# Order of the first loads and place of the second layer's constants in the spectral stage of a two-layer metaformer kernel

## The chip, the cores and the metric

The kernel runs on one core of one Trainium2 chip. The metric is the device time of one execution in microseconds, given as the median of three runs. The profile is one further execution; its own time stands in the table below. A difference under 0.2% (some 5 us here) can hardly be told from no change.

## The reference, cut to what matters

The input is a batch of 8 images with 128 channels and 32 by 32 positions, which become 1024 tokens per image. Layer 0 is a row attention and then a spectral unit (STU). Layer 1 is a deformable convolution along rows and then a mixture of eight experts.

```python
x = x + _L0_conv_ref(_ln_c(x), ...)            # attention, softmax over one row of 32 keys
t = _to_tokens(x)
t = t + _L0_ffn_ref(_ln_t(t), sigma, phi, M_u, M_phi_plus, M_phi_minus, log_weights, gumbel)
x = x + _L1_conv_ref(_ln_c(x), conv_w, ...)    # gather at learned offsets, 3 taps
t = t + _L1_ffn_ref(_ln_t(t), router_w, ...)   # top 2 of 8 experts
```

The change lies in how the spectral unit starts. The spectral unit convolves the tokens causally with 16 filters (the columns of `phi`), for even and odd time steps, multiplies each result by 128 by 128 matrices (`M_phi_plus`, `M_phi_minus`, weighted by `sigma` and by a choice of four resolutions), and adds three plain lags with the matrices `M_u`. The kernel writes the convolution as products with Toeplitz blocks of the filter.

## The kernel before, in words

**Stages.** `attention_bounded` (from line 500) runs first, for all eight images, and stores its result in DRAM as `x1d` (line 688). Then `spectral_and_second_layer` (line 1589) runs everything else in one order that is written out by hand: Tile keeps this order on every engine (`manual_schedule`). The spectral products and the second layer of the image before are interleaved there.

**The loop.** The work is a list of 128 pairs n = (image b, filter k), 16 filters for each of 8 images. Each pair has two halves, `src` 0 and 1, and each half two slots. In a half, `filter_image` (line 1514) makes three groups of matrix products: `p_x` in slot 0, `p_y` in slot 1, `p_z` after it. ScalarE copies `p_x` out (lines 1555, 1556), GpSimd adds the copies into `part` (line 1557), VectorE adds `part` to `p_y` and `p_z` (lines 1562, 1565, 1572). The filter of a pair is the tile `teto` (three buffers), its block differences are `diff` (lines 1299 and 1300, on GpSimd). `mix` (line 1509) then multiplies the convolved tokens `us` with the matrices `mf` and sums in PSUM (`po`). Pair m = n-2 is mixed in half 0 (its term 1), pair m = n-1 in half 1 (its term 0). So the first mix stands in half 1 of pair 1 and needs `mf` of pair 0.

**The matrices.** For the first 16 pairs `mf` is made on the core: `load_parts` (line 1426) brings both source matrices into one buffer, `m_room`; `terms` (lines 1431, 1432, GpSimd) makes their sum and difference, `both`, in one buffer; `weigh` (lines 1439 and 1441, VectorE) makes `mf`, which is also stored to DRAM (line 1444). `between` sets when: after half 0 of pair n come the differences of filter n+1 and `weigh(n)`; after half 1 come `terms` for pair n+1 and the load of `m_room` for pair n+2. Pair 0 is special: `terms(0)` comes after its half 0, `weigh(0)` and `terms(1)` after its half 1. At the end of a pair the filter for n+3 is loaded.

**Side work.** `rows[0]` is a queue of generators. `advance` (line 1611), called after every slot, adds 3.2 units to a budget and runs steps of the generator at the head until the budget is spent; a step costs what it yields, or 1 unit. So a pair has 12.8 units. The queue starts with `channels` of image 0 (line 1460: transposes `p_ut`, memset and copies into `ut`, which has one buffer), and `layer.setup()` (line 821), which makes the second layer's constants in 22 steps: ten small loads into `gw` (lines 830 to 843), three into `bias` (847, 849), memsets and iotas (851 to 864), twelve stores of zeros into `tab` (871), `shift` tiles, `cb`, `rw`, `rb`, `ew`, and eight small loads into `ebm` (902). At pair 1 `begin(1)` is put behind it: `prepare(1)`, then the `channels` of image 1. `add_lags` (line 1497) multiplies `ut` of image 0 by the lag matrices `mu` in half 1 of pair 2. The second layer of image 0 starts after pair 17.

**Queues.** All direct loads and stores are issued by SyncE (SP) in program order. The program gives SP's transfers eight completion semaphores in turn, so a transfer is issued only when the one eight places before it has landed. `prepare` (line 1446) issues a gather of `x1` on GpSimd. Before the loop SP issues, in this order, `teto` of pairs 1 and 2 (the filter of pair 0 was read during the attention), the four loads of `mu`, and `m_room` of pair 0.

Of the kernel before, what the change touches and what calls it, by code (L numbers as in the profile page):

```python
# [1587 lines left out]

def spectral_and_second_layer(tc, spec, layer, weights):
    work = [(b, k) for b in range(B) for k in range(NF)]  # L1590
    imgs = {0: spec.prepare(0)}
    filters = {0: spec.given.filter, 1: spec.load_filter(1), 2: spec.load_filter(2)}
    less = {0: spec.given.given.diff}
    spec.load_lags()

    mf = {}
    parts = spec.load_parts(0)
    both = None

    rows = [deque([spec.channels(imgs[0], layer.bank), layer.setup()]), deque()]
    starts = {}
    todo = [0.0, 0.0]

    def second_layer(b, x1):
        got = []
        yield from layer.points(b, imgs[b]["x2"], got, False, x1)
        rows[1].append(layer.sampled(b, got, False))

    def advance(time):
        for r, row in enumerate(rows):
            todo[r] = todo[r] + time if row else 0.0
            while todo[r] > 0 and row:
                took = next(row[0], row)
                if took is row:
                    row.popleft()
                else:
                    todo[r] -= took or 1.0

    def between(n, src):

        nonlocal parts, both
        if src == 0 and n + 1 < len(work):
            less[n + 1] = spec.differences(filters[n + 1])
        if n == 0:
            if src == 0:
                both = spec.terms(parts)
                parts = spec.load_parts(1)
                return  # L1630
            mf[0] = spec.matrices()
            spec.weigh(0, both, mf[0])
        elif n < NF and src == 0:
            mf[n] = spec.matrices()
            spec.weigh(n, both, mf[n])
        if src == 1 and n + 1 < NF:
            both = spec.terms(parts)
            if n + 2 < NF:
                parts = spec.load_parts(n + 2)
        if n in (0, 1) and src == 1 - n:  # L1640
            spec.lags(weights, range(2 * n, 2 * n + 2))

    sums = {}
    for n in range(len(work) + 2):
        now = work[n] if n < len(work) else None
        if now is not None:
            b, k = now
            if k == 1 and b + 1 < B:  # L1650
                starts[b + 1] = spec.begin(b + 1, layer.bank, imgs)
                rows[0].append(starts[b + 1])
            elif k == 0 and b:
                for _ in starts[b]:
                    pass
            us = sums[n] = spec.sb.tile([C, 2, 2, HT], F32, tag="us", name="us", bufs=3)
        for src in range(2):
            run = iter(())
            if now is not None:
                run = spec.filter_image(imgs[b], src, filters[n], less[n], us, layer.bank)  # L1660
            for slot, spans in enumerate((SPANS[0:3], SPANS[3:4])):
                next(run, None)
                m = n - 2 + src
                if 0 <= m < len(work):
                    img, k = imgs[work[m][0]], work[m][1]
                    if src == 1 and slot == 0 and k == 0:
                        spec.start_sums(img)
                    if src == 1 and slot == 0 and k == NF - 3:
                        img["tokens"] = layer.residual(img["b"])
                    if src == 1 and slot == 0 and k == 1:  # L1670
                        spec.add_lags(img)
                    spec.mix(img, 1 - src, spans, mf[m], sums[m], k == NF - 1)
                    if src == 0 and slot == 1 and k == NF - 1:
                        spec.finish(img)
                        if img["b"] + 1 < B:
                            rows[0].appendleft(second_layer(img["b"], img["tokens"]))
                if now is not None:
                    advance(RATE if b + 1 < B else LAST_RATE)
            next(run, None)
            if now is not None:  # L1680
                between(n, src)
        if n + 3 < len(work):
            filters[n + 3] = spec.load_filter(work[n + 3][1])
        if NF <= n + 2 < len(work):
            mf[n + 2] = spec.read_matrices(work[n + 2][1])

    last = imgs[B - 1]
    runs = [layer.image(B - 1, last["x2"], last["tokens"]), chain(*rows[0], *rows[1])]
    while runs:
        runs = [r for r in runs if next(r, r) is not r]  # L1690
# [3 lines left out]
def metaformer_kernel(  # L1694
# [41 lines left out]
    with tc.manual_schedule(engines=None):  # L1736
        spectral_and_second_layer(tc, spec, layer, weights)
# [50 lines left out]
```

## Time and profile before

| what | value |
|---|---|
| median of three runs | 2662.8 us (2657.89 to 2663.11) |
| profiled execution | 2658.17 us, of which the span is 2656.4 us |
| TensorE busy | 2500.7 us, 94% |
| VectorE, ScalarE, GpSimd busy | 1852.6, 1064.2, 1449.2 us |
| mean granted TensorE clock | 0.978 |
| attention's last TensorE work | ends at 908.57 us of the span |
| first product of the spectral stage | 911.79 us |

Each engine runs its own instructions in order, and the page gives its busy time. An idle time stands in square brackets behind an instruction in the timeline, with the work that ended it. TensorE's products are the longest row, so its idle times in the span and its granted clock tell where time is lost.

### The profile page before, as it was taken

The page shows a single profiled execution, that of the slowest core. Times are in us where ns is not written, and L with a number is a line of the kernel's source. Part 1 is how long each engine was busy: PE and PEld are TensorE (multiplying, and loading weights), DVE is VectorE, ACT ScalarE, POOL GpSimd, SP SyncE. Part 2 cuts the span into 40 slices and gives each one's busy share as a digit, 9 for nine tenths or more (in the row PEclk, how much of TensorE's full clock was granted, in tenths as well). Part 3 has the DMA queues.
Part 4 walks back from the last instruction along what each step waited for, and adds up shares of the span by engine and source line. Part 5 has one row for each costly group of instructions (what it writes and reads, how often), then busy time and mean ns, then how long its engine had stood idle before and what let it go on. Part 6 is the DMA issues. An engine that isn't in the chain of part 4 may idle for free. (4 is left out here: it accounts for less than half of the span.)

```text
span 2656.4 us, 47332 instructions
## 1 busy us (share of the span) xinstructions
PE 2500.7 (94%) x18768; PEld 1750.2 (66%) x18768; DVE 1852.6 (70%) x2800; ACT 1064.2 (40%) x1982; POOL 1449.2 (55%) x1535
## 2 busy tenths in 40 slices
PE   6999999999999789999999999999999999999924
PEld 3555555555555468878778778778778778778612
DVE  3788888888888545549749748658658658658656
ACT  4676766667766311124214214224224224224222
POOL 4777777877778555446246237237337337236230
PEclk9999999999999999999999999999999999999966
DMA  1000000000000154465365266266356357256160
GB/s 30 2 18 2 18 17 2 18 2 18 10 18 18 57 165 157 145 191 176 99 189 180 91 182 192 87 183 188 98 168 201 100 154 215 92 144 213 48 182 20
DMA packets 214531, 271.29 MB, mean 102 GB/s; under 512 B 20948, under 2 KB 147092, under 8 KB 214304
## 3 DMA queue, kind: packets, MB, share of 16 engines
q1 hardware_dynamic: 197504, 212.61, 26.6%
q0 software_dynamic: 16800, 55.59, 6.3%
q8 instruction: 150, 2.46, 0.4%
q14 instruction: 77, 0.63, 0.1%
HBM read 200.22 MB, written 67.92 MB: 101 GB/s over the span
## 5 line engine op out<-in xcount | busy, mean ns | idle before, releaser
L623 POOL TENSOR_TENSOR t<-e 128x1024 f32<-128x1024 f32 x256 | 608.2, 2376 | 198.9 <-ACT e L614 198.7
L651 DVE TENSOR_TENSOR e<-e,rb 128x2048 f32<-128x2048 f32 x256 | 570.8, 2277 | 84.5 <-PE rb L644 84.5
L614 ACT ACTIVATE e<-s 128x2048 f32<-128x2048 f32 x256 | 481.1, 1879 | 253.0 <-PE s L609 250.5
L1557 POOL TENSOR_TENSOR part<-us,part 128x256 f32<-128x256 f32 x256 | 191.0, 746 | 705.6 <-ACT part L1556 698.7
L1509 PE MATMUL po<-us,mf 128*128 128x128 f32 (+2 forms) x2048 | 528.1, 381 | 5.8 <-DVE mf L1441 5.8
L1555 ACT COPY us<-p_x 128x256 f32<-128x256 f32 x256 | 95.2, 372 | 753.8 <-PE p_x L1544 740.6
L1562 DVE TENSOR_TENSOR part<-p_y,part 128x512 f32<-128x512 f32 x256 | 175.3, 685 | 289.3 <-PE p_y L1544 200.2
L1509 PEld LDWEIGHTS po<-us,mf 128*128 128x128 f32 x2048 | 308.8, 191 | 37.8 <-DVE mf L1441 6.2
L609 PE MATMUL s<-q,k 32*128 32x256 f32 x4096 | 295.9, 403 | 15.2 <-ACT e L614 14.4
L661 PE MATMUL av<-e,vt 128*32 128x256 f32 x4096 | 288.2, 389 | 4.0 <-DVE e L651 2.7
L1572 DVE TENSOR_TENSOR us<-p_z,part 128x512 f32<-128x512 f32 x256 | 174.8, 683 | 159.3 <-PE p_z L1544 159.2
L609 PEld LDWEIGHTS s<-q,k 32*128 32x128 f32 x4096 | 186.4, 185 | 137.9 <-ACT e L614 116.6
L1544 PEld LDWEIGHTS p_z<-diff,gap 128*128 128x128 f32 x1024 | 191.9, 189 | 125.3 <-issue 87.5
L1544 PE MATMUL p_z<-diff,gap 128*128 128x256 f32 x1024 | 263.4, 379 | 3.1 <-DVE base L907 3.1
L661 PEld LDWEIGHTS av<-e,vt 128*32 128x32 f32 x4096 | 101.4, 109 | 141.6 <-issue 84.7
L1091 POOL DMA_INDIRECT g<-tab,here x168 | 165.9, 988 | 43.2 <-issue 37.0
L1109 ACT ACTIVATE g<-g,w 128x128 f32<-128x128 f32 x448 | 140.1, 393 | 74.2 <-DMA g<-tab,here 73.2
L1299 POOL TENSOR_TENSOR diff<-teto 128x516 f32<-128x516 f32 x127 | 165.0, 1299 | 2.2 <-DMA teto<-in_phi_o 1.4
L1117 DVE TENSOR_REDUCE x<-g 128x128 f32<-128x1536 f32 x56 | 158.7, 2834 | 5.0
L637 DVE RECIPROCAL r<-z 128x256 f32<-128x256 f32 x64 | 112.5, 1757 | 71.3 <-PE z L630 71.1
L1544 PE MATMUL p_y<-diff,gap 128*128 128x256 f32 x512 | 152.9, 380 | 2.4 <-POOL diff L1299 2.3
L1544 PE MATMUL p_x<-teto,ht 128*128 128x256 f32 x512 | 131.4, 379 | 0.0
(268 smaller groups left out, 3708.9 us busy)
## 6 DMA issues: line engine op xcount, KB each, us to landing
mf<-mfd SPq DMA_DIRECT2D x112, 512.0 KB
tab<-gs SPq DMA_DIRECT2D x192, 256.0 KB
teto<-in_phi_o SPq DMA_DIRECT2D x127, 256.5 KB
teto<-in_phi_e SPq DMA_DIRECT2D x127, 256.0 KB
mfd<-mf SPq DMA_DIRECT2D x16, 512.0 KB
xc<-in_x SPq DMA_DIRECT2D x8, 512.0 KB
x1d<-xt SPq DMA_DIRECT2D x8, 512.0 KB
m_room<-in_M_plus SPq DMA_DIRECT2D x16, 256.0 KB
```

The costliest lines, as they stand in the source:

```text
L609: nc.tensor.matmul(s[:, j, c, :], img["k"][rows, hg, 2 * r + c, :], q[rows, qc * QU : (qc + 1) * QU], start=True, stop=True,)
L614: nc.scalar.activation(e.rearrange("p j c q -> p (j c q)"), s.rearrange("p j c q -> p (j c q)"), AF.Exp, scale=float(HD) ** -0.5,)
L623: nc.gpsimd.tensor_add(t, e[:, :, 0, :], e[:, :, 1, :])
L651: nc.vector.tensor_tensor(e, e, un["rb"].unsqueeze(2).to_broadcast([P, NH, 2, QU]), ALU.mult)
L661: nc.tensor.matmul(qrt["av"][32 * j : 32 * j + 32, 0:QU], img["v"][:, 2 * r + c, P * hg + 32 * j : P * hg + 32 * j + 32], un["e", r][:, j, ...
L1091: nc.gpsimd.indirect_dma_start(out=tiles[-1][:, tap].rearrange("p k c -> p (k c)"), out_offset=None, in_=rows[tap], in_offset=bass.Indirec ...
L1299: lambda: nc.gpsimd.tensor_sub(blocks[:, :, 0:2], pair, one),
L1509: self.nc.tensor.matmul(out, lhsT, rhs, start=bank not in img["opened"], stop=last, skip_group_check=True)
L1544: nc.tensor.matmul(out, weights, moving, start=start, stop=stop, skip_group_check=True)
L1557: nc.gpsimd.tensor_add(part[:, 0], mine[:, :, 0:P], part[:, 1])
L1562: nc.vector.tensor_tensor(part[:, 2:4], y[:, 0].unsqueeze(1).to_broadcast([C, 2, 2, P]), part[:, 0:2], ALU.add)
L1572: nc.vector.tensor_tensor(result(2, 4), z, part[:, 2:4], ALU.add)
```

## The change

The loads ahead of the loop are put in another order. `load_parts(0)` comes first, then the filter of pair 1, then `prepare(0)` and the four loads of `mu`, and the filter of pair 2 last. In `rows[0]` a generator that yields 40.0 once stands between `channels` of image 0 and `layer.setup()`, so that 40 units of the budget pass with no step. Nothing is added to or left out of the computation. Everything behind the filler in `rows[0]` moves with it: the constants now start in half 0 of pair 3 and end in half 1 of pair 4, `prepare(1)` stands in half 1 of pair 4 and `channels` of image 1 in half 0 of pair 5. Before, the constants ran from half 0 of pair 0 to half 1 of pair 1, and `channels` of image 1 in half 1 of pair 1 and half 0 of pair 2.

```diff
 def spectral_and_second_layer(tc, spec, layer, weights):
     work = [(b, k) for b in range(B) for k in range(NF)]
-    imgs = {0: spec.prepare(0)}
-    filters = {0: spec.given.filter, 1: spec.load_filter(1), 2: spec.load_filter(2)}
-    less = {0: spec.given.given.diff}
-    spec.load_lags()
 
     mf = {}
     parts = spec.load_parts(0)
     both = None
-
-
-
-    rows = [deque([spec.channels(imgs[0], layer.bank), layer.setup()]), deque()]
+    filters = {0: spec.given.filter, 1: spec.load_filter(1)}
+    less = {0: spec.given.given.diff}
+    imgs = {0: spec.prepare(0)}
+    spec.load_lags()
+    filters[2] = spec.load_filter(2)
+
+
+
+    rows = [deque([spec.channels(imgs[0], layer.bank), iter([40.0]), layer.setup()]), deque()]
     starts = {}
     todo = [0.0, 0.0]
```

## The prediction

> **What bounds the kernel.** I read the page first.
>
> ```profile
> span 2656.4 us, 47332 instructions
> PE 2500.7 (94%) x18768; PEld 1750.2 (66%) x18768; DVE 1852.6 (70%) x2800; ACT 1064.2 (40%) x1982; POOL 1449.2 (55%) x1535
> PE   6999999999999789999999999999999999999924
> ```
>
> TensorE (PE) is the long row. Of its 40 slices of 66.4 us it has one dip inside the span, the 14th and 15th, where attention ends and the spectral stage begins. The table of stretches, for PE alone, cuts this start:
>
> ```profile
> core 0: us, PE busy (x), PEclk, DMA share, GB/s
> 911.80:926.70 14.90, 14.89 (x68) 0.89 0.74 212
> 926.70:932.50 5.80, 0.00 (x0) 0.72 0.12 1
> 932.50:936.10 3.60, 3.57 (x10) 0.50 0.22 56
> 936.10:946.10 10.00, 8.47 (x43) 1.00 0.83 262
> 946.10:949.20 3.10, 0.04 (x1) 1.00 1.03 274
> 949.20:953.20 4.00, 3.99 (x11) 0.57 0.61 233
> 961.00:1095.00 134.00, 134.00 (x622) 1.00 0.52 165
> 1095.00:2500.00 1405.00, 1392.66 (x6452) 1.00 0.50 154
> ```
>
> PE idles 5.8 us, 1.5 us inside the fourth row, and 3.1 us, and runs two pieces at about half clock. From 961 to 2500 it idles 12.3 us of 1539. What is won at the start should therefore stay won. The timeline names the causes:
>
> ```profile
> 919.10 1.28 POOL L1299 TENSOR_TENSOR diff<-teto 128x516 f32<-128x516 f32 x1 [0.28 <-DMA teto<-in_phi_o]
> 925.84 1.27 POOL L1431 TENSOR_TENSOR both<-m_room 128x512 f32<-128x512 f32 x1 [4.76 <-DMA m_room<-in_M_minus]
> 929.87 0.40 SPq L1426 DMA_DIRECT2D m_room<-in_M_plus  x1
> 932.53 2.08 PE L1509 MATMUL po<-us,mf 128*128 128x128 f32 x6 [5.84 <-DVE mf L1441]
> 938.55 1.26 POOL L1431 TENSOR_TENSOR both<-m_room 128x512 f32<-128x512 f32 x1 [8.87 <-DMA m_room<-in_M_minus]
> 958.98 0.59 ACT L1471 COPY ut<-p_ut 128x512 f32<-128x512 f32 x1 [27.87 <-PE po L1509]
> ```
>
> PE's first mix waits for `mf` of pair 0, that for `both`, that for `m_room`, which stood last on SP. The next `m_room` needs 8.7 us from issue to use. ScalarE stands 27.9 us before image 1's `ut` copy, since `ut` has one buffer and image 0's lags come later. The transfers of 928 to 935 us show why the second `m_room` is late, and 921 to 924 us give the rate of 512-byte pieces:
>
> ```profile
> DMA packets 913, 0.03 MB, mean 4 GB/s; under 512 B 903, under 2 KB 903, under 8 KB 913
> ...
> DMA packets 2079, 1.04 MB, mean 345 GB/s; under 512 B 77, under 2 KB 2074, under 8 KB 2079
> ```
>
> For 7 us almost nothing moved but the constants' 4-byte pieces (`bias`), with `m_room` already issued behind them.
>
> **What the Trainium skill says.** "DMA: Bandwidth & Descriptors", Queues, rings and completion order: the transfers of one issuer share one row of rings, and each DMA engine takes descriptors in ring order. The 7 us above agree. The same page, Rules for kernel authors: a strided last dimension becomes one descriptor per element; `bias` and `gw` agree (903 pieces under 512 B). "TensorE: Matmul & The Clock Gate", What's actually happening: after an idle window of about 3.4 us the clock halves until a busy one has passed. The trace half agrees: 3.1 us of idle time was enough at 946, the 1.43 us at 941 to 943 was not. The same page's section on the array's architecture calls ACT and DVE strict FIFO; the ScalarE line shows it.
>
> **The change part by part.** All on the profiled execution, in its microseconds.
>
> *SP's first issue.* `teto` waited 2.9 us for the landing of `x1d` by the waits of SP, and went at 913.46. `m_room` now takes the place in SBUF where `x1` stood, so it may not have that wait; no engine starts the stage before 911.8. Between 911.8 and 913.5 I take 913.0.
>
> *`m_room` first.* It is 1024 pieces of 512 B: 1.5 us at 2079 pieces in 3 us. `teto` of pair 1 was released at 919.1 after an issue at 913.46; now 1.5 later for `m_room` and 0.5 earlier for the issue: 920.1 (918.9 to 921.1, if the `x1` gather hits it for half a microsecond more). On GpSimd, in order: `diff` 1.28 + 0.74, `both` 1.27 + 1.26 (`m_room` landed long before), `part` 0.72: 920.1 + 2.0 + 2.5 + 0.7 = 925.3. Before, from that `part`'s end at 929.0 to PE's mix at 932.53 took 3.5 us (VectorE's three adds and `weigh`). So the mix comes at 928.8 (927.6 to 929.8); PE runs out of work at 926.7 as before, and idles 2.1 us instead of 5.8. A half-clock window of 3.4 us costs 1.7; with 2.1 between the two gaps above I take half of it, 0.9 (0 to 1.7).
>
> *`mu` and the second filter behind.* `mu` (1536 pieces, 2.3 us) lands by about 923.5, the filter (3 to 4 us) by about 928. VectorE wants `mu` after `weigh`, at 928.8, GpSimd the filter after about 931. Cost nothing; were that cover gone, each would cost its own lateness. `prepare(0)` stays first on GpSimd's stage: nothing.
>
> *Constants away from pairs 0 and 1.* GpSimd's 2.9 us of memsets and iotas lay under the wait for `teto`: nothing. But SP now issues the second `m_room` right after `both`, about 924.7, behind the filter of pair 2: it lands by about 929.5, when `weigh(0)` ends (928.8). So `both(1)` ends by 932, `part` by 932.7, VectorE's adds of pair 1 half 0 by 934.4, `weigh(1)` by 936.3, the last lag scaling by 937.6. PE after its mix at 928.8 needs these PSUM banks from 933 (`p_y` of pair 2) on and the scaled `mu` at 939.2: no wait longer than a few tenths.
>
> *Image 1's `channels` moved.* ScalarE is no longer stuck. Two groups of `p_ut` (0.9 + 1.0 us of PE) leave this stretch and return in pair 5: zero in sum, but the comparison has to take it out.
>
> *Sum of the start.* The common mark is the lag product, at 953.56 before. From mix to mark lie two halves of 5.19 us (the period of `p_x` in the steady stretch): 928.8 + 10.4 + 0.9 = 940.1. Gain 953.56 - 1.9 - 940.1 = 11.6 us; with the ends above 9.8 to 13.7.
>
> *Constants in pairs 3 and 4.* Count from the start of pair 3; pair 5 starts at +20.8, pair 6 at +33.0 (two times 5.19, and `p_ut`'s 1.9). SP: `teto(5)` at +1 (3 to 4 us of pieces), the ten `gw` loads (4 us, by 924 to 928), the `mfd` store at +7.8 (1.3 us), three `bias` loads (7.2 us) to about +17.5, twelve `tab` stores, 396 pieces (about 5 us), to +22.5; only then `m_room(5)` (1.5 us, 1 to land, 1.3 for the `x1` gather beside it) to +26, and `teto(6)` to +30. Unhindered, `m_room(5)` would be issued at about +10.5 and wanted at +18.3. So `both(5)` is 8 us late. Behind it on GpSimd stand `part` of pair 5 and `diff(6)`; behind `part`, VectorE's adds. PE asks for the bank of pair 5's first `p_y` in pair 6's `p_y`, at +34.8; 26 + 2.5 + 0.7 + 1.1 = +30.3. It asks for `teto(6)` at +33.0; that is there at +30. Six PSUM banks, three `us` and three `teto` hide it, with some 3 us to spare. The later `ew`, `ebm` and `m_room(6)` fall in a queue that is emptying. I take 1.0 us for this (0 to 8: `bias` twice as slow takes the 3 us and 4 more, and a half-clock window), so the gain is 10.6.
>
> Profiled: 2658.2 - 10.6 = 2647.6. The profiled execution is 4.6 us under the median, so the median goes from 2662.8 to 2652.2. Its own range, from the ends above and the runs' own spread of some 2 us either way, is 2648 to 2656.
>
> **Rivals.**
>
> *The constants give part of it back.* `bias` under a loaded queue holds SP longer than its 7.2 us, and PE waits in pairs 5 and 6 for `teto` or a bank. For it: the issue order, and one landed wait of 8.9 us before. Against it: the 3 us to spare. Stall 3 to 9 us: 2654 to 2661.
>
> *Slower.* The same place, but longer: PE waits at `p_x` of pair 6 for `teto(6)`. It decides once `teto(6)` lands later than +33 + 11.6 = +45, that is, once the constants hold the queue 15 us longer than the 21 us counted, for instance with `bias` at a third of its rate. Each microsecond beyond counts in full, and the idle time adds half-clock windows: with 18 us, 2668. Against it: alone, `bias` needed 7.2 us.
>
> *Absorbed.* A later stage sets its own pace (the gathers of the second layer, or the tail after 2500, where PE is busy 67 of 156 us), or the first filter swaps places with `m_room` as the late load: `diff` at 925.8 would put the mix at 934.6, and the freed second `m_room` alone would still bring some 6 us. 2656 to 2663. Against it: PE's 12.3 us of idle time in 1539.
>
> **How the numbers follow.** Likeliest 0.60 (of it 0.04 within 0.2%, by the spread of the medians), partly given back 0.15 (half faster, half within), absorbed 0.12 (0.04 faster, 0.08 within), slower 0.13. A measurement here tells about 0.2%, 5.3 us, from no change. Faster: 0.56 + 0.075 + 0.04 = 0.675; within: 0.04 + 0.075 + 0.08 = 0.195; slower 0.13. The range reaches up through the absorbed case to 2664 and leaves most of the slower case out; down to 2646 for the best ends and a low run.
>
> **What would show it.** Right: `both` at about 922 instead of 925.8; the first mix near 929; no ScalarE wait of 28 us; the lag product near 940; 4-byte pieces and a late `both` in pairs 3 to 5, with PE unbroken there; and everything after shifted by the same 10 us. Wrong: a PE wait on `teto` or a `p_y` bank 25 to 35 us after pair 3 starts, half-clock windows there, or `diff` released later than 922 at the start.

## The result, and the profile after

The changed kernel took 2653.0 us (median of nine runs, 2650.94 to 2654.23), the kernel before in the same comparison 2660.05 us (nine runs, 2657.8 to 2663.26). The ratio is 0.9972, with a 95% interval of 0.9964 to 0.9981: faster by 7.05 us, or by 5 to 9.6 us with the interval. A later comparison with nineteen runs of the changed kernel gave 0.9977, 5.4 us by the medians. The time foretold, 2652.2 us, is 0.8 us off, and that is luck: the gain foretold, 10.6 us, is 3.5 us too large, and what hid this was the starting point, for the three runs of before had a median of 2662.8 us and the nine runs 2660.05 us.

The profiled execution took 2652.63 us, where 2647.6 had been foretold. These lines of its page answer to those of before: span, busy times, and TensorE's 40 slices.

```profile
span 2650.9 us, 47334 instructions
...
PE 2504.3 (94%) x18768; PEld 1753.2 (66%) x18768; DVE 1859.3 (70%) x2800; ACT 1064.3 (40%) x1982; POOL 1447.5 (55%) x1535
...
PE   6999999999999899999999999999999999999924
```

The dip of two slices (7 and 8 tenths before) has become one 8. The digits alone prove little, since a second profile of the kernel before shows a single 7 there. The timeline of the changed kernel around it follows; columns are the start, the busy time, the engine, the line and the tiles, and in square brackets the idle time before and what ended it.

```profile
914.10 0.38 SPq L1426 DMA_DIRECT2D m_room<-in_M_plus  x1
...
915.07 0.50 SPq L1317 DMA_DIRECT2D teto<-in_phi_e  x1
...
923.76 1.27 POOL L1299 TENSOR_TENSOR diff<-teto 128x516 f32<-128x516 f32 x1 [7.13 <-DMA teto<-in_phi_o]
...
925.68 1.27 POOL L1431 TENSOR_TENSOR both<-m_room 128x512 f32<-128x512 f32 x1
...
932.39 2.07 PE L1509 MATMUL po<-us,mf 128*128 128x128 f32 x6 [3.61 <-DVE mf L1441]
...
932.47 1.32 POOL L1431 TENSOR_TENSOR both<-m_room 128x512 f32<-128x512 f32 x1 [3.61 <-DVE mf L1441]
...
944.36 5.38 PE L1509 MATMUL po<-ut,mu 128*128 128x128 f32 x24
...
977.49 0.59 ACT L1471 COPY ut<-p_ut 128x512 f32<-128x512 f32 x1 [1.12 <-PE p_ut L1467]
```

The first `both` no longer waits for `m_room`, but GpSimd reaches it only at 925.68, since `diff` in front of it now waits for its filter until 923.76. The second `both` (938.55 before, after 8.87 us of waiting for a transfer) waits for nothing but the first `weigh`. The wait of 27.87 us on ScalarE is gone: its copy for image 1 now waits 1.12 us.

Executions start the spectral stage at slightly different times, so the profiles are compared from the stage's first product on (911.79 us before, 912.85 after). This table has the starts after that product in us. The lag product is that of `add_lags`; the last column is the start of VectorE's copy of image 0's finished sums (line 1586), which waits for the mixes of all 16 pairs.

| kernel | `diff` | first `both` | second `both` | first mix | lag product | end of image 0's mixes |
|---|---|---|---|---|---|---|
| before | 7.31 | 14.04 | 26.76 | 20.74 | 41.77 | 201.50 |
| before, again | 7.39 | 13.91 | 26.44 | 20.61 | 41.17 | 200.91 |
| changed | 10.91 | 12.83 | 19.62 | 19.54 | 31.51 | 192.48 |
| changed, again | 11.73 | 13.66 | 20.44 | 20.36 | 32.54 | 193.51 |
| changed, third profile | 10.77 | 12.70 | 19.47 | 19.39 | 31.42 | 192.39 |
| order alone | 11.09 | 13.01 | 27.10 | 19.72 | 40.41 | 200.15 |
| delay alone | 6.18 | 13.52 | 20.30 | 20.22 | 33.25 | 194.21 |
| gather left out | 9.78 | 11.70 | 18.49 | 18.41 | 30.59 | 191.56 |
| filter first | 8.21 | 11.11 | 17.90 | 17.83 | 31.28 | 192.25 |
| terms first | 11.60 | 5.17 | 17.86 | 17.78 | 28.26 | 189.23 |
| terms first, two gathers out | 9.48 | 4.90 | 15.74 | 15.66 | 26.14 | 187.11 |
| the same, again | 10.14 | 5.27 | 16.39 | 16.32 | 26.80 | 187.77 |

"Before" and "order alone" have 1.9 us of `p_ut` ahead of the lag product that the others do later. With that taken off, the changed kernel is 8.4 us ahead at the lag product, and 9.0 us at the end of image 0's mixes. Profiles of one and the same kernel differ here by up to 1.1 us, so smaller differences between rows say nothing.

### The profile page after: what moved, and what is told of

It reads as the page before. It is cut to its first block, busy times and chain, and to the rows that moved or that the text cites. A ratio compares the mean times of both kernels' runs of the same rounds, so it can differ in the third digit from the quotient of the medians.

```text
span 2650.9 us, 47334 instructions
## 1 busy us (share of the span) xinstructions
PE 2504.3 (94%) x18768; PEld 1753.2 (66%) x18768; DVE 1859.3 (70%) x2800; ACT 1064.3 (40%) x1982; POOL 1447.5 (55%) x1535
## 5 line engine op out<-in xcount | busy, mean ns | idle before, releaser
L1299 POOL TENSOR_TENSOR diff<-teto 128x516 f32<-128x516 f32 x127 | 164.4, 1295 | 10.6 <-DMA teto<-in_phi_o 9.2
L1544 PE MATMUL p_z<-teto,ht 128*128 128x256 f32 x512 | 131.7, 380 | 0.0
```

Source lines behind the costliest of these rows:

```text
L1299: lambda: nc.gpsimd.tensor_sub(blocks[:, :, 0:2], pair, one),
L1544: nc.tensor.matmul(out, weights, moving, start=start, stop=stop, skip_group_check=True)
```

## The experiments

**Each part alone.** `order_only` is the changed kernel without the filler; `delay_only` is the kernel before with it.

```diff
 # order_only, against the changed kernel
-    rows = [deque([spec.channels(imgs[0], layer.bank), iter([40.0]), layer.setup()]), deque()]
+    rows = [deque([spec.channels(imgs[0], layer.bank), layer.setup()]), deque()]
 # delay_only, against the kernel before
-    rows = [deque([spec.channels(imgs[0], layer.bank), layer.setup()]), deque()]
+    rows = [deque([spec.channels(imgs[0], layer.bank), iter([40.0]), layer.setup()]), deque()]
```

> The new order of the first loads alone, without the filler of 40 units. Theory (the constants ahead of the second m_room cost most): TensorE's first mix comes some 1 us earlier than before, counted from the stage's first product (19.5 to 20 us instead of 20.7), the second both on GpSimd still waits 7 us or more for its m_room, ScalarE still stands some 28 us before image 1's ut copy, and the time is 1 to 2 us under the kernel before. Rival (the late first m_room cost most): the time is 5 us or more under it.

> The filler of 40 units alone, with the old order of the first loads. Theory: the first mix stays where it was (20.7 us after the first product, with 5 to 6 us of idle TensorE before it), but the second both waits less than 1 us for its m_room, the long ScalarE wait is gone, and the lag product comes 6 to 7 us earlier when the moved p_ut is taken out; time 5 to 7 us under the kernel before. Rival: the time is only 1 to 2 us under it, since the first m_room is as late as it was.

`order_only` took 2662.45 us beside 2662.57 us of before: ratio 1.0001, 0.9993 to 1.0009, no difference that these runs can tell. `delay_only` took 2657.26 us beside the same: 0.9982, 0.9973 to 0.9991. At the end of image 0's mixes the order alone is 1.35 us ahead of before, the delay alone 7.3 us, both 9.0 us. So most of the gain comes from the filler, that is, from moving the constants and image 1's `channels` out of the stage's first pairs. The times agree, but do not prove it by themselves, for the intervals of `delay_only` and of the changed kernel overlap. The timelines tell why. First that of `order_only`:

```profile
938.72 1.26 POOL L1431 TENSOR_TENSOR both<-m_room 128x512 f32<-128x512 f32 x1 [10.23 <-DMA m_room<-in_M_minus]
...
957.45 0.59 ACT L1471 COPY ut<-p_ut 128x512 f32<-128x512 f32 x1 [27.52 <-PE po L1509]
```

and that of `delay_only`:

```profile
925.20 1.27 POOL L1431 TENSOR_TENSOR both<-m_room 128x512 f32<-128x512 f32 x1 [5.38 <-DMA m_room<-in_M_minus]
...
931.98 1.33 POOL L1431 TENSOR_TENSOR both<-m_room 128x512 f32<-128x512 f32 x1 [3.61 <-DVE mf L1441]
```

With the constants in place, the second `m_room` still lands behind their pieces (10.23 us of waiting), and ScalarE still stands 27.52 us before image 1's `ut`. With the constants away, the first `m_room` is as late as ever (5.38 us), but the second is there when `weigh` is done.

The filler moves two things at once, and no run moves one without the other: the constants, which hold up the second `m_room`, and image 1's `channels`, which hold up ScalarE. The first profile of before shows which of them TensorE felt:

```profile
941.76 0.69 DVE L1562 TENSOR_TENSOR part<-p_y,part 128x512 f32<-128x512 f32 x1 [8.30 <-POOL part L1557]
...
942.92 1.13 PE L1467 MATMUL p_ut<-flip,ht 128*128 128x128 f32 x8 [1.43 <-DVE us L1565]
...
949.21 1.52 PE L1544 MATMUL p_z<-diff,gap 128*128 128x256 f32 x4 [3.07 <-DVE base L907]
...
960.11 0.70 PE L1544 MATMUL p_y<-teto,xc 128*128 128x256 f32 x2 [0.28 <-ACT ut L1473]
```

TensorE's waits of 1.43 and 3.07 us are for VectorE, which had stood 8.30 us for `part` on GpSimd, behind the late second `both`. Its only wait for ScalarE was 0.28 us. So the late `m_room` explains these waits and ScalarE's long wait hardly any, by reading the trace and not by an experiment.

**What the first mix waits for.** In the changed kernel TensorE still idles 3.61 us before it. One kernel leaves out the gather of `x1` of image 0; the other leaves out those of images 0 and 1 and also puts the first `terms` ahead of the first differences. No instruction reads these two gathers.

```diff
 # no_gather, in prepare; terms_first_no_gather has "if b > 1:"
+        if b:
-        img["x1"] = sb.tile([P, NT, C], F32, tag="x1", name="x1")
+            img["x1"] = sb.tile([P, NT, C], F32, tag="x1", name="x1")
 ...
 # terms_first_no_gather, in between
+        if n == 0 and src == 0:
+            both = spec.terms(parts)
+            parts = spec.load_parts(1)
+            less[1] = spec.differences(filters[1])
+            return
         if src == 0 and n + 1 < len(work):
             less[n + 1] = spec.differences(filters[n + 1])
         if n == 0:
-            if src == 0:
-                both = spec.terms(parts)
-                parts = spec.load_parts(1)
-                return
```

> The changed kernel without the gather of x1 for image 0, whose values no instruction reads (this load is left out, nothing else). Theory (the gather takes the DMA engines while the first filter comes in, so that its 512 KB took 5 us and not 4): diff on GpSimd starts 2 to 2.6 us earlier, counted from the first product (8.3 to 8.9 us instead of 10.9), the idle time before the first mix falls from 3.6 to about 1 us, and the time is 2 to 4 us under the changed kernel, so 9 to 11 under the kernel before. Rival (the filter's loads are slow by themselves, or by the mu loads behind them): diff within 0.5 us of where it was, time as the changed kernel's, 7 us under the kernel before.

> The changed kernel without the x1 gathers of images 0 and 1 (left out; nothing reads them), and with terms of pair 0 ahead of the differences of pair 1 on GpSimd, so that both no longer stands behind the wait for the filter. Theory: TensorE does not idle before its first mix (under 0.5 us) and no half clock follows, 11 to 13 us under the kernel before. Rival: the differences are then late for TensorE's p_y of pair 1, which waits 2 us or more in place of the mix; 7 to 9 us under the kernel before.

Without the gather, `diff` and all that follows come 1.1 us earlier after the first product, half of what was expected, and TensorE still idles 2.54 us. Since the profiles of the changed kernel alone differ by 1 us here, the time from SP's first issue to `diff` is the better measure: 8.3 to 8.6 us in the three profiles without the gather, 9.1 to 10.1 us in the seven that have it and `m_room` first. The time is 2654.89 us, ratio to before 0.9969, 0.9958 to 0.9981, which is not told apart from the changed kernel. With both edits `both` starts at 4.90 us, the mix at 15.66 us and without idle time, and image 0's mixes end 5.4 us ahead of the changed kernel's; 2653.06 us, ratio 0.996, 0.9947 to 0.9972, some 10 us under before where 11 to 13 were expected. From the start of `diff` to the mix it is 8.63 us in the changed kernel and 6.18 us here: the 2.45 us between them are the two instructions of `both`, which no longer stand behind `diff`.

**The constants under the steady stretch.** These two ask what hides them. `bias_three_times` issues the three small loads of `bias` two more times, into tiles that nothing reads; `filler_16` makes the filler 16 units instead of 40, so that the constants come about two pairs earlier.

```diff
 # bias_three_times, in setup
+            for n in range(2):
+                more = cp.tile([P, 9], F32, name=f"bias_again{n}")
+                for xy in range(2):
+                    nc.sync.dma_start(
+                        more[:, 3 * xy : 3 * xy + 3], off_rb[xy].partition_broadcast(P)
+                    )
+                nc.sync.dma_start(more[:, 6:9], mask_b.partition_broadcast(P))
 # filler_16
-    rows = [deque([spec.channels(imgs[0], layer.bank), iter([40.0]), layer.setup()]), deque()]
+    rows = [deque([spec.channels(imgs[0], layer.bank), iter([16.0]), layer.setup()]), deque()]
```

> The changed kernel with the three bias loads issued three times in all, the extra ones into tiles that nothing reads. Theory (the queue has about 4 us to spare in pairs 3 to 6, and bias blocks it 7.2 us each time): m_room of pair 5 lands 14 to 15 us later than in the changed kernel, about +40 us from the start of pair 3, the filter of pair 6 some 3 us later still, and TensorE waits 9 to 11 us at the first products of pair 6, with half clock after it; 11 to 14 us over the changed kernel, so 4 to 7 us over the kernel before. Rival (the buffers hide far more, or the queue recovers): no TensorE wait over 2 us there and a time within 2 us of the changed kernel's.

> The changed kernel with a filler of 16 units in place of 40, so that the constants run in pairs 1 to 3 behind the second and third m_room, and image 1's channels in pair 3, after image 0's lag product. Theory (the constants only have to stay behind the m_room that GpSimd waits for, and image 1's channels behind the lags): no TensorE wait over 1 us in pairs 1 to 5, the lag product within 1.5 us of the changed kernel's (31.5 us after the first product), time within 3 us of the changed kernel's. Rival (only the pure TensorE stretch of the lags gives the cover): a late both of pair 3 stops TensorE 3 us or more in pair 3 or 4.

First the same place in the changed kernel. Of the stretches for TensorE alone (time, its length, busy time and instructions, granted clock as a share of full speed, then the transfers), these two begin with pair 3:

```profile
953.90:995.00 41.10, 41.10 (x200) 1.00 0.63 173
995.00:1095.00 100.00, 100.00 (x463) 1.00 0.51 163
```

and in its timeline the steps of the forecast are:

```profile
974.10 0.40 SPq L1426 DMA_DIRECT2D m_room<-in_M_plus  x1
...
979.70 1.26 POOL L1431 TENSOR_TENSOR both<-m_room 128x512 f32<-128x512 f32 x1 [5.46 <-DMA m_room<-in_M_minus]
...
982.87 1.28 POOL L1299 TENSOR_TENSOR diff<-teto 128x516 f32<-128x516 f32 x1
...
986.83 1.03 PE L1544 MATMUL p_x<-teto,xc 128*128 128x256 f32 x4
```

`both` of pair 5 was late (5.46 us on GpSimd), at +25.8 from the start of pair 3. `teto` of pair 6 was there by +29.0 at the latest, since `diff` did not wait for it, and TensorE asked for it at +32.9. TensorE never stopped. `bias_three_times` took 2664.36 us beside 2659.51 us of before, ratio 1.0017, 1.001 to 1.0024. Its timeline:

```profile
970.76 17.54 SPq L878 DMA_DIRECT2D tab<-zero  x12
...
988.40 0.40 SPq L1433 DMA_DIRECT2D m_room<-in_M_plus  x1
...
995.92 2.04 PE L1551 MATMUL p_x<-teto,xc 128*128 128x256 f32 x4 [10.73 <-DMA teto<-in_phi_o]
```

Pair 3 starts at 952.10 there, so `m_room` was issued at +36.3 instead of +20.2: the two added sets held the queue 16 us longer, 8 us a set. TensorE then waited 10.73 us for `teto` of pair 6, with half clock behind it (0.56 over the next 7.1 us), and the kernel fell behind before, by 0.17%. The cover is real, and it is finite.

`filler_16` took 2653.68 us, ratio 0.9977, 0.997 to 0.9984, which is also the ratio of the changed kernel's nineteen runs. In its timeline two `both` are late,

```profile
954.54 1.26 POOL L1431 TENSOR_TENSOR both<-m_room 128x512 f32<-128x512 f32 x1 [7.88 <-DMA m_room<-in_M_minus]
...
969.23 1.27 POOL L1431 TENSOR_TENSOR both<-m_room 128x512 f32<-128x512 f32 x1 [7.18 <-DMA m_room<-in_M_minus]
```

and in its stretches TensorE does not notice:

```profile
932.40:960.00 27.60, 27.60 (x137) 1.00 0.52 138
960.00:1095.00 135.00, 135.00 (x626) 1.00 0.55 175
```

SP's issues show where the constants stand there:

```profile
925.02 0.38 SPq L1426 DMA_DIRECT2D m_room<-in_M_plus  x1
...
932.17 0.37 SPq L1426 DMA_DIRECT2D m_room<-in_M_plus  x1
...
934.16 0.43 SPq L830 DMA_DIRECT2D gw<-in_conv_w  x1
```

These are the second and the third `m_room`, and the first constant behind them, still in pair 1. So the constants need not leave the first two pairs. It is enough that they stand behind the second and third `m_room`, and image 1's `channels` behind the lag product; how far behind made no difference between these two kernels.

**Where some 4 us went in the first profile of the changed kernel.** Counted from the first product, it is still 9.1 us ahead near 2110 us of the span, 8.7 us near 2316 us, and 5.1 us at the last `p_x`, near 2510 us; the span is 5.5 us shorter. Between the last two lies a stretch at half clock that the first profile of before does not have. One theory is that the changed start shifts TensorE against something and brings this stretch; the other that it comes and goes by itself. `before_again` and `after_again` are the two kernels with nothing edited.

> The kernel before once more, for one profile. Theory (the half-clock windows after 2300 us come by the place of a short wait in the clock's windows, by chance, and not by the change): the profile can hold such windows between 2300 and 2470 us though the first one held none, with the stage up to 2100 us as it was. Rival (only the changed start brings them): none there.

> The changed kernel once more, for one profile. Theory: the half-clock window of 6.8 us at 2454 us is not there or lies elsewhere or has another length; the stretch from the first product to the end of image 0's mixes takes 192.5 us again, within 1.5 us, 8 to 10 us less than before. Rival: the same window of 6.8 us at the same place.

The single executions took 2664.05 and 2657.09 us. The stretches for TensorE alone, first of `before_again`,

```profile
2465.00:2468.00 3.00, 1.69 (x7) 1.00 0.03 14
2468.00:2473.00 5.00, 4.75 (x14) 0.66 0.00 0
```

then of `after_again`,

```profile
2318.00:2323.00 5.00, 4.55 (x11) 0.66 0.00 0
...
2461.00:2467.00 6.00, 5.71 (x21) 0.72 0.00 0
```

of the changed kernel's first profile,

```profile
2454.60:2461.50 6.90, 6.37 (x18) 0.52 0.01 3
```

and of the first profile of before:

```profile
2459.70:2467.00 7.30, 5.74 (x28) 1.00 0.05 19
```

The kernel before has the stretch too in its second profile, and the changed kernel has one of about 3.4 us instead of 6.8 us at this place in its second, and another at 2319 us. All of them have the same wait of 2.33 or 2.34 us for `diff` near 2460, and in part some shorter ones around it, the first profile of before as well, where the clock stayed at 1.00. So the change isn't needed for such a stretch, and in a single profile it is chance: the two profiles of the kernel with terms first and two gathers out, between which nothing was edited, had 10.2 us at half clock between 2300 and 2500 us and none. Whether the change makes the stretches more frequent stays open. The two profiles of before have 0 and 3.4 us of them, the three of the changed kernel 6.8, 6.8 and 10.3 us.

**Which of the two first loads should come first.** `filter_first` puts the filter of pair 1 ahead of `m_room` and leaves the rest of the change. `terms_first` keeps the loads of the change and only puts the first `terms` ahead of the differences (the second half of the diff above). `terms_first_no_gather_2` and `after_timed` repeat earlier kernels, so that all four are timed side by side.

```diff
 # filter_first
+    filters = {0: spec.given.filter, 1: spec.load_filter(1)}
     parts = spec.load_parts(0)
     both = None
-    filters = {0: spec.given.filter, 1: spec.load_filter(1)}
```

> The changed kernel with the filter of pair 1 ahead of the first m_room; nothing else moved. Theory (GpSimd takes the differences first, and m_room ahead of the filter delays them by its own time and its issue): diff starts 6.9 to 7.6 us after the first product (10.9 to 11.7 in the changed kernel), both at 9.5 to 10.5 (12.8), the first mix at 16 to 17.2 with less than 1.5 us of idle TensorE before it, and image 0's mixes end 2 to 4 us earlier than in the changed kernel. Rival (what lands first is set by all the bytes in flight): both still starts at 12 us or later and nothing is gained.

> The changed kernel with terms of pair 0 ahead of the differences of pair 1 on GpSimd; the gathers stay. Theory: both starts some 5 to 6.5 us after the first product, diff where it was (about 11), the first mix 1 to 2.5 us earlier than in the changed kernel, with about 1.2 us of idle TensorE, and a wait of up to 0.5 us for diff at pair 1's p_y. Rival: diff is later than it was and p_y waits 2 us or more.

> Both edits together once more (the x1 gathers of images 0 and 1, which nothing reads, are left out), beside the changed kernel on the same chip: 3 to 5 us under the changed kernel, 10 to 12 under the kernel before.

> The changed kernel itself, to be compared with the three others of this call: 0.9964 to 0.9981 of the kernel before again.

| kernel | median, us | ratio to before (2662.07 us) | 95% interval |
|---|---|---|---|
| changed | 2656.68 | 0.9977 | 0.997 to 0.9984 |
| filter first | 2654.95 | 0.9971 | 0.9959 to 0.9983 |
| terms first | 2651.38 | 0.9961 | 0.9947 to 0.9974 |
| terms first, two gathers out | 2648.63 | 0.9958 | 0.9944 to 0.9971 |

GpSimd's timeline in `filter_first`:

```profile
921.25 1.28 POOL L1299 TENSOR_TENSOR diff<-teto 128x516 f32<-128x516 f32 x1 [3.65 <-DMA teto<-in_phi_o]
...
924.16 1.28 POOL L1431 TENSOR_TENSOR both<-m_room 128x512 f32<-128x512 f32 x1 [0.94 <-DMA m_room<-in_M_minus]
```

and in `terms_first`:

```profile
916.48 1.27 POOL L1431 TENSOR_TENSOR both<-m_room 128x512 f32<-128x512 f32 x1 [1.11 <-DMA m_room<-in_M_minus]
...
922.92 1.27 POOL L1299 TENSOR_TENSOR diff<-teto 128x516 f32<-128x516 f32 x1 [3.93 <-DMA teto<-in_phi_o]
```

In `filter_first` the filter is in use 6.19 us after its issue (915.06), as against 9.66 us from SP's first issue in the changed kernel: `m_room` ahead of it cost 3.5 us. The mix came 1.7 us earlier for it, but 6.8 us at half clock went with it:

```profile
930.10:936.90 6.80, 6.03 (x14) 0.50 0.46 157
```

At the lag product only 0.2 us was left, where image 0's mixes had been expected 2 to 4 us earlier, and in time this kernel is not told apart from the changed one. `terms_first` shows the other way out: the load that is first on SP should also be the one whose consumer is first on GpSimd. Its mix comes 1.8 us earlier, with 1.3 us of idle time instead of 3.6 and no half clock there, and its lag product 3.3 us earlier. With the gathers gone as well, the waits of TensorE hold for `mf`

```profile
PE po L1510 <- DVE mf L1441: 0.4, 1, 0.4
```

that is, one wait of 0.4 us; in its first profile there was none. That version beats both kernels. It is 0.42% under before by the ratio. Against the changed kernel it is 8 us ahead by the medians and 5 us by the ratios; the two intervals overlap by a ten-thousandth, but four of its five runs lie below the lowest of the nineteen runs of the changed kernel (2651.74 us). Of `terms_first`, three of five do.

## Why the prediction was right, and where it was not

**The direction and the place** were right. The gain lies in the start of the stage, later work keeps it, and the constants cost nothing where they now stand. `order_only` and `delay_only` also show which of the two edits carries it, which the sum had not separated: it gave 3.7 us to the first mix, and the changed kernel's mix is only 1.2 us earlier (20.74 to 19.54 us). What came after the mix made the rest, and by the trace of before that was the second `m_room` far more than ScalarE's wait. One of the prediction's own signs of being wrong did come: `diff` was released at 923.76, later than 922, and past it also when counted from the first product. Of its signs of being right, `both` at about 922, the mix near 929 and the lag product near 940 did not come (925.68, 932.39 and 944.36). The stage started 1.06 us later in this profile, which explains a third of these differences at most.

**SP's first issue** was foretold 1.2 us after the first product and came 1.25 us after it. That it fits is luck: the two other profiles of the changed kernel have 1.72 and 1.15 us, the kernel before 1.67 us, and the reason given was wrong. SP's waits in the changed kernel hold

```profile
SPq L1426 <- DMA x1d<-xt: 2.6, 1, 2.6
```

so `m_room` still waited 2.6 us for that landing, as `teto` did before (2.9 us).

**`m_room` first** is the step that failed by size. From SP's first issue to `diff` the forecast has 7.1 us (5.6 and 1.5 for `m_room`); it was 9.66 us. `m_room` ahead cost 3.5 us instead of 1.5, by `filter_first`; 0.97 us of it is the time between SP's issues at 914.10 and 915.07, which the sum left out. The other half microsecond lies between `filter_first` (6.19 us) and before (5.64 us). The `x1` gather, allowed half a microsecond in the range, was some 1.1 us by `no_gather`. So `teto` came at +10.9 instead of +8.3, past the bound, and the chain behind it took its foretold length (8.63 us; foretold 8.7). The mix was 2.5 us late by that.

**The half clock** after the idle time was taken at 0.9 us and was a whole stretch, about 1.6 us lost:

```profile
932.30:935.50 3.20, 3.11 (x9) 0.51 0.42 169
```

The idle time was 3.6 us instead of 2.1. In all eleven profiles with 2.5 us or more of idle time ahead of the first mix a stretch at half clock followed or began in it, in the three with 1.3 us or less none did; 2.1 us lies between and was not met. From mix to lag product it was 11.97 us instead of 11.3. The two misses, 2.5 and 0.7 us, make up the whole 3.2 us by which the start gained less (8.4 instead of 11.6 us, outside the bounds of 9.8 to 13.7).

**The constants in pairs 3 and 4** went nearly by the numbers: `both` of pair 5 foretold at +26 and found at +25.8, `teto` of pair 6 foretold at +30 and there by +29.0, asked for at +32.9 (foretold +33.0). The 1.0 us allowed for it was 0.

**The rivals.** That the constants give part back is refuted by the unbroken 41.1 us. The slower case did not happen, but its place and mechanism are those of `bias_three_times`: TensorE waits at `p_x` of pair 6 for `teto`. The deciding point was put at 15 us of longer holding; at 16 us the kernel is 0.17% slower than before, so with the smaller gain the true point lies lower, near 11 us if each microsecond counts in full. Of the absorbed case one half came true: the filter took the place of `m_room` as the late load. The 6 us that it left to the second `m_room` agree with `delay_only`, 6.6 us at the lag product. In the change this happened in part, so the gain of 7 us fell between that rival's 6 and the 10.6 of the likeliest case.

**Left open:** between the first and later profiles of one and the same kernel some microseconds differ away from the start (`before` and `before_again` have spans of 2656.4 and 2662.3 us); the half-clock stretches are a part of it, and the rest was not traced. Of the 3.5 us that `m_room` cost the filter, 1.5 us is its own transfer at the rate foretold and 0.97 us issue time. The last microsecond may be the gather, which with `m_room` first falls on the filter: from 917.6 to 920 us of the changed kernel's span GpSimd's queue moved 0.30 MB and SP's only 0.16 MB. No run leaves out the gather with the filter first, so this isn't shown.

## What to carry to other kernels

Where two loads feed one chain and an engine runs their consumers in order, the order of the loads and the order of the consumers should agree: moving one load ahead makes the other the late one. Here it was worth 3.3 us at the lag product to swap the consumers, and 0.2 us to swap the loads, in one profile each; in the second, 6.8 us at half clock took part of what was won. Look then at the next buffer of the same kind, whose load may stand behind bulk work on the queue; here, taking that work away, together with image 1's `channels`, was worth 7 of the 9 us. Small loads with many tiny pieces belong under a stretch with buffers to spare, and adding such pieces, as `bias_three_times` did, measures how much is to spare.

## What the runs showed of the hardware

- TensorE's half-clock stretches at the first mix and between 2300 and 2500 us each lasted 3.4 or 6.8 us, in all fourteen profiles. At the first mix, idle times of 2.54 to 5.84 us brought one each time and idle times up to 1.30 us none, but the length did not follow the idle time: 2.92 us went with 6.8 us, 3.75 us with 3.4 us. Between 2300 and 2500 us, one kernel had 10.2 us of them in one execution and none in another. The Trainium skill, "TensorE: Matmul & The Clock Gate", What's actually happening, puts the window at some 3.4 us and calls it free-running, with results that vary by run. The lengths and the variation agree; an idle time shorter than a window, 2.54 us, was enough here.
- `m_room` ahead of the filter on one queue cost 3.5 us, for 0.5 MB that at the 345 GB/s of before would be 1.5 us.
- A gather on GpSimd's queue that nothing waits for cost SP's filter some 1.1 us: the time from SP's first issue to `diff` was 8.3 to 8.6 us without it and 9.1 to 10.1 us with it.
- A set of three `bias` loads of 1.5 KB each, in small pieces, held SP's queue for 8 us.
